# Preparation results of the attention in the attention's own PSUM bank, drained at the head of the next scan part

## The chip, the cores and the metric

The kernel runs on one core of a Trainium2 chip, in one launch. The metric is device time in microseconds (us); the times of a kernel are medians of several runs. A profile is one execution recorded by the hardware profiler. The engines are named as the profile names them: PE (TensorE, matmuls) with PEld (its weight loads), DVE (VectorE), ACT (ScalarE), POOL (GpSimd), and SP, whose queue issues the DMAs.

## What is computed

The input is x, 8 images of 256 channels and 48 x 48 pixels (2304 tokens). Two layers follow one another, each added to its input. Layer 0 is an attention over each token's 16 most similar tokens, layer 1 is two Mamba blocks.

```python
# layer 0: x = x + conv0(gn(x))
feat_pos = tokens @ W.T + bias
feat = feat_pos[:, :, :c]
pos = feat_pos[:, :, c:]
norm = jnp.linalg.norm(pos, axis=-1, keepdims=True)
pos = pos / jnp.maximum(norm, 1e-12)
sim = jnp.einsum('bnc,bmc->bnm', pos, pos)
topksim, topkid = jax.lax.top_k(sim, K)              # K = 16
attn = jax.nn.softmax(topksim, axis=-1)
out = jnp.einsum('bnk,bnkc->bnc', attn, topkfeat)
...
# layer 1: x = x + conv1(gn(x)), for each of DEPTH = 2 blocks
xn = _layernorm(xf, ...)
xi, z = in_proj(xn); xc = silu(conv(xi)); dt, Bm, Cm = x_proj(xc)
dt = jax.nn.softplus(...)
h = h * jnp.exp(dt * A) + dt * B_t * x_t             # over the 2304 tokens
y = jnp.einsum('bds,bs->bd', h, C_t) + xc * Dp
out = (y * silu(z)) @ out_w
```

## The kernel before

**Scan parts.** Layer 1 is the frame of the program. Tokens are cut into 6 chunks of 384, and a chunk of one of the two blocks is a *unit*: 12 units an image. A unit's 512 inner channels with 16 states each are cut into 16 *steps* of 32 channels (128 partitions with four states on each), and a step is scanned in two *parts* of two states. So an image has 384 parts and the program 3072. In each part ACT makes two decays (`decay`, L828, an exponential into one of two pairs of PSUM banks, called `da` in the profile), DVE runs one `tensor_tensor_scan` (L843), and either DVE (L845) or POOL (L871, `pool_part`) multiplies the states with C. POOL makes B times x for each step two steps ahead (L804). `sum_states` (L886, L889) sums the states of four steps over partitions on PE into a tile `y`.

**The order.** The main loop runs over parts m and writes the order out by hand; each engine works through its instructions in that order. A part m holds, in this order: `carry(m - 1)` and `decay(m + 1)`; at an even part POOL's products and `take_up`, at an odd one `carry_pool`; the unit's other pieces that the table `between` gives to this part (`inner`); `run_scan(m)`; the pieces of the table `behind` (`outer`); and last one piece of layer 0, by `ahead.go(m)`. The tables give each piece a part counted from its unit's first, with negative numbers for what comes ahead: input projection (`in_proj`, tile `pe`), the convolution's `tap` and `taps`, `silu_x`, `x_proj`, `softplus` with the step-size matmuls `step_size` (tile `pd`), the copies of z and `silu_z`, the layer norm (`mean`, `variance`, `root`, `root_end`, `spread_root`, `scale`), `gate`, `out_proj` (tile `pw`) and `leave`.

**Layer 0 beside the scan.** `layer0` is a generator; each `yield` ends what it puts into one part. The first image's layer 0 runs alone, before the scan (`alone`). For each of the other seven, `Ahead` runs it while the image before is scanned: it starts 42 parts ahead of that image's first scan (at part 342 of the image still being scanned) and has to be done 384 parts later. It is made of

- the *preparation*: group norm statistics over x (`group_stats`, tiles `pm` and `pv`), then for each chunk two projections `pp` (256 position channels), three feature products `pf`, the squared norms `pn`, and, for the chunk before, the inverse norms spread over all partitions (`spread`, tile `pb`) with which DVE scales `pos` (L298). ACT drains `pp` (L337, and L341 squares), `pf` (L346) and `pn` (L351);
- the *attention*: 18 blocks of 128 tokens by the table `within`, 16 parts apart, starting at a fixed part in 16. The preparation's last `yield` hands over the number of the first part, and `go` waits for the part that fits.

**PSUM.** Of the eight banks four hold decays, three make up the tag `mm`, and one is the tag `po`, in which the attention sums the weighted features of a block (`weigh`, L462). All other matmul results of layer 1 take `mm` (helper `mm`), and so do those of layer 0 (helper `mm0`), which are the preparation's `pm`, `pv`, `pp`, `pf`, `pn`, `pb` and the attention's `psim`, `pt`, `pr`. A matmul that needs a bank of a tag with none free waits until the last reader of the earliest one has gone by.

**When a preparation result is drained.** `step(make, use)` takes a matmul and its drain. It makes the matmul and keeps the drain in `pending`; beside the scan, at most one is kept (`depth` is 1). The next `step`, one part later and again at that part's end, runs the kept drain first and then its own matmul.

Of the kernel before, what the change touches and what calls it, by code (L numbers as in the profile page):

```python
# [8 lines left out]
F32 = mybir.dt.float32  # L9
# [6 lines left out]
P = 128  # L16
# [9 lines left out]
def tile_conv_preact(  # L26
# [19 lines left out]
    B, C, N = x.shape  # L46
# [7 lines left out]
    T = 384  # L54
    NCH = N // T
    TB = T // P
# [125 lines left out]
    def group_stats(st, found, mm0, name):  # L182


        mv = small.tile([P, CB, 2], F32, tag="gn_mv", name=f"mv_{name}")
        for cb in range(CB):
            nc.vector.bn_aggr(mv[:, cb, :], st[:, cb])
        yield
        pm = mm0(CB, f"pm_{name}")
        nc.tensor.matmul(pm, group, mv[:, :, 0], start=True, stop=True)  # L190
        yield
        mean = small.tile([P, CB], F32, tag="gn_mean", name=f"mean_{name}")
        nc.scalar.copy(mean, pm)
        yield
        q = small.tile([P, CB], F32, tag="gn_q", name=f"q_{name}")
        nc.gpsimd.tensor_sub(q, mv[:, :, 0], mean)
        nc.gpsimd.tensor_mul(q, q, q)
        nc.gpsimd.tensor_add(q, q, mv[:, :, 1])
        yield
        yield  # L200
        pv = mm0(CB, f"pv_{name}")
        nc.tensor.matmul(pv, group, q, start=True, stop=True)
        yield
        rstd = small.tile([P, CB], F32, tag="gn_rstd", name=f"rstd_{name}", bufs=4)
        var = small.tile([P, CB], F32, tag="gn_var", name=f"var_{name}")
        nc.scalar.copy(var, pv)
        rsqrt_start(rstd, var, eps5)
        yield
        rsqrt_end(nc.gpsimd, rstd, var, 1e-5, name)
        shift = small.tile([P, CB], F32, tag="gn_shift", name=f"shift_{name}", bufs=4)  # L210
        nc.gpsimd.tensor_mul(shift, mean, rstd)
        nc.gpsimd.tensor_scalar(shift, shift, -1.0, None, ALU.mult)
        found.extend((rstd, shift))
        yield

    def spread(cols, n, psum, name):

        pb = psum(n * P, name)
        for j in range(n):
            nc.tensor.matmul(  # L220
                pb[:, j * P : (j + 1) * P], cols[:, j : j + 1].to_broadcast([P, P]), ident,
                start=True, stop=True,
            )
        return pb
# [2 lines left out]

    def layer0(b, left, pool, ps0, alone):  # L230
        def mm0(w, name):
            return ps0.tile([P, 512], F32, tag="mm", name=name, bufs=5 if alone else 3)[:, :w]

        more = 2 if alone else 1
        depth = 2 if alone else 1
        pending = []

        def step(make, use):

            if len(pending) == depth:  # L240
                leave_psum()
            pending.append((make(), use))

# [5 lines left out]
        st = small.tile([P, CB, NCH, 6], F32, tag="gn_st0", name=f"st0_{b}")  # L249
# [15 lines left out]
            yield  # L265
        found = []
        nxt = load_chunk(pool, x[b], 0, "x", f"xt_{b}_0", 3 * more)
        yield from group_stats(st, found, mm0, f"a{b}")
        rstd, shift = found
        pos = pool.tile([P, CB, N], F32, tag="pos", name=f"pos_{b}", bufs=1)  # L270
        feat = pool.tile([P, NB, C], F32, tag="feat", name=f"feat_{b}", bufs=1)
# [21 lines left out]
        def scale(c):  # L293


            def use(pb):
                cs = slice(c * T, (c + 1) * T)
                nc.vector.tensor_tensor(  # L298
                    pos[:, :, cs], pos[:, :, cs], pb.unsqueeze(1).to_broadcast([P, CB, T]), ALU.mult
                )  # L300

            step(lambda: spread(rn[c], TB, mm0, f"pb_{b}_{c}"), use)

        def chunk(c, xn):
            cs = slice(c * T, (c + 1) * T)

            def project(ob):
                pp = mm0(T, f"pp_{b}_{c}_{ob}")
                for k in range(CB):
                    nc.tensor.matmul(  # L310
                        pp, w0_sb[:, k, C + ob * P : C + (ob + 1) * P], xn[:, k, :],
                        start=(k == 0), stop=(k == CB - 1),
                    )
                return pp

            def features(j):
                pf = mm0(C, f"pf_{b}_{c}_{j}")
                for k in range(CB):
                    nc.tensor.matmul(
                        pf, xn[:, k, j * P : (j + 1) * P], w0_sb[:, k, 0:C],  # L320
                        start=(k == 0), stop=(k == CB - 1),
                    )
                return pf

            def norms():
                pn = mm0(TB, f"pn_{b}_{c}")
                for j in range(TB):
                    for k in range(CB):
                        nc.tensor.matmul(
                            pn[:, j : j + 1], sq[:, k, j * P : (j + 1) * P], ones_col,  # L330
                            start=(k == 0), stop=(k == CB - 1),
                        )
                return pn

            def position(ob):
                def use(pp):
                    nc.scalar.activation(  # L337
                        pos[:, ob, cs], pp, AF.Identity, bias=b_pos[:, ob : ob + 1]
                    )
                    if ob == CB - 1:  # L340
                        nc.scalar.activation(sq, pos[:, :, cs], AF.Square)  # L341

                return use

            def feature(j):
                return lambda pf: nc.scalar.copy(feat[:, c * TB + j, :], pf)  # L346

            def norm(pn):
                n2[c] = small.tile([P, TB], F32, tag="n2", name=f"n2_{b}_{c}")

                nc.scalar.activation(n2[c], pn, AF.Relu, bias=tiny[:, 0:1])  # L351

            for ob in range(CB):
                step(lambda: project(ob), position(ob))
                yield
            if c > 0:
                inverse_norm(c - 1)
            for j in range(TB):
                step(lambda: features(j), feature(j))
                yield  # L360
                if j == 0 and c > 0:
                    inverse_norm_end(c - 1)
            step(norms, norm)
# [3 lines left out]
        for c in range(NCH):  # L367
            yield from chunk(c, xn)
            if c + 1 < NCH:
                xn = normalized(c + 1)  # L370
            yield
            if c > 0:
                scale(c - 1)
                yield
        while pending:
            leave_psum()
# [2 lines left out]
        yield  # L379
        inverse_norm_end(NCH - 1)  # L380
        yield
        yield
        scale(NCH - 1)
        yield
        leave_psum()
        yield
# [131 lines left out]
                f(t, *args)  # L518
            yield
        found = []  # L520
        yield from group_stats(st1, found, mm0, f"b{b}")
        left.update(x1=x1, rstd=found[0], shift=found[1])

    lefts = [{} for _ in range(B)]
    with tc.tile_pool(name="first", bufs=1) as pool0, tc.tile_pool(
        name="first_ps", bufs=1, space=PSUM
    ) as ps0:
        for _ in layer0(0, lefts[0], pool0, ps0, True):
            pass


# [132 lines left out]
    def scale(unit):  # L664
        v = unit["v"]
        nc.vector.tensor_tensor(  # L666
            v, v, unit["lb"].unsqueeze(1).to_broadcast([P, CB, T]), ALU.mult
        )
# [204 lines left out]
    def carry_pool(n):  # L873

        if not 0 <= n < NSTEP:
            return
        unit, i, k = at(n)
        lo = [p for p in range(PARTS) if on_pool(unit, i, p)]
        if lo and unit["c"] + 1 < NCH:
            qs = slice(lo[0] * HQ, (lo[-1] + 1) * HQ)  # L880
            nc.scalar.copy(h_st[:, unit["d"], i, qs], unit["bx"][i][:, qs, T])
# [78 lines left out]
    class Ahead:  # L960
# [3 lines left out]

        def turn(self, image):
            self.image, self.begun, self.started = image + 1, None, False
            self.run = iter(())
            if self.image < B:
                self.run = layer0(self.image, lefts[self.image], keep, ps, False)

        def finish(self, image):
            while self.image <= image:
                for _ in self.run:
                    pass
                self.turn(self.image)

        def go(self, m):
            if self.image == B:
# [9 lines left out]
    ahead = Ahead()  # L988
    first = min(part for part, *_ in between + behind)
    last = max(part for part, *_ in between + behind)  # L990
    for m in range(first, PARTS * NSTEP - HOOKS + last + 1):
        n, p = divmod(m, PARTS)
        carry(m - 1)
        decay(m + 1)
        if p == 0:
            make_bx(n + LEAD)
            pool_part(n - 1)
            take_up(n + 1)
        else:
            carry_pool(n - 1)  # L1000
        for f, unit, args in inner.get(m, ()):
            if f is load_v:
                ahead.finish(unit["b"])
            f(unit, *args)
        run_scan(m)
        for f, unit, args in outer.get(m, ()):
            f(unit, *args)
        ahead.go(m)
# [41 lines left out]
```

## Time and profile before

| | |
|---|---|
| median of 3 runs | 9901.13 us (9897.18 to 9910.42) |
| the profiled execution | 9898.83 us |
| its span | 9897.1 us |
| mean granted PE clock | 0.889 of full speed |
| scan, DVE L843, both forms | 5330.6 us busy, 3072 times |
| decays, ACT L828 | 3591.0 us busy, 6144 times |
| B times x, POOL L804 | 5298.4 us busy, 1536 times |
| products with C, POOL L871 | 3303.6 us busy, 1320 times |
| preparation's drains on ACT, L337, L341, L346, L351 | 160.3 us busy, 336 times |
| preparation's scaling on DVE, L298 | 45.3 us busy, 48 times |

The busy share of an engine is a mean over stages. A row of waits names the instruction that waited, who released it, and the total; a timeline row has the start, the time taken (of the whole run of like instructions, where it says x4), and in brackets how long the engine had been idle before it and for whom. The tail of a name says what is written and read: `pf<-w,xt` is a matmul of weights and tokens into the tile `pf`.

### The profile page before, as it was taken

What the parts mean: (1) busy time and instruction counts of PE and PEld (TensorE: products, weight loads), DVE (VectorE), ACT (ScalarE), POOL (GpSimd) and SP (SyncE); (2) the same over time, 40 slices, a digit from 0 to 9 for tenths busy, and PEclk for the clock granted to TensorE, in tenths of its full rate; (3) what the DMA queues carried; (4) which work ended last, traced back from release to release, by engine and by line L of the source; (5) the groups of instructions that cost most, each with busy time, mean ns of one, the idle gap of its engine ahead of it and who ended that gap; (6) DMA issues with size and microseconds to landing.
All of it is one profiled execution on the core that took longest, in us unless ns stands there. A gap on an engine that the chain in (4) does not pass through costs nothing. (4 is left out here: it accounts for less than half of the span.)

```text
span 9897.1 us, 133780 instructions
## 1 busy us (share of the span) xinstructions
PE 8000.3 (81%) x36736; PEld 4388.5 (44%) x36736; DVE 8956.8 (90%) x7993; ACT 7322.2 (74%) x15966; POOL 8943.3 (90%) x3927
## 2 busy tenths in 40 slices
PE   8878887788878888788877888778887788866665
PEld 6644544444534454445444445344544444522222
DVE  4589998999989999899998999899998999988998
ACT  4477777778777877777877787777787778766766
POOL 0099999999989999899998999999998999999999
PEclk9989998899989998899988999889998899977777
DMA  1144445444444444444454444444445444444544
GB/s 32 37 133 126 134 130 152 124 132 129 136 142 131 129 134 137 140 126 133 130 148 128 130 128 134 144 132 125 135 128 152 121 133 127 138 136 129 145 138 122
DMA packets 1243503, 1271.37 MB, mean 128 GB/s; under 512 B 266592, under 2 KB 1215840, under 8 KB 1242752
## 3 DMA queue, kind: packets, MB, share of 16 engines
q1 hardware_dynamic: 1230496, 1262.45, 44.7%
q8 instruction: 293, 4.80, 0.2%
q14 instruction: 458, 3.75, 0.1%
q10 hardware_dynamic: 12256, 0.36, 0.1%
HBM read 1048.94 MB, written 212.86 MB: 127 GB/s over the span
## 5 line engine op out<-in xcount | busy, mean ns | idle before, releaser
L804 POOL TENSOR_TENSOR bx<-BC,dtxr 128x1536 f32<-128x1536 f32 x1536 | 5298.4, 3453 | 115.6 <-PE y L889 59.8
L828 ACT ACTIVATE da<-dtr,A_sb 128x385 f32<-128x385 f32 x6144 | 3591.0, 585 | 871.6 <-DVE bx L843 558.0
L843 DVE TENSOR_TENSOR_SCAN bx<-da,bx 128x770 f32<-128x770 f32 x2040 | 3521.8, 1746 | 190.5 <-ACT da L828 151.4
L871 POOL TENSOR_TENSOR bx<-bx,BC 128x1536 f32<-128x1536 f32 (+1 forms) x1320 | 3303.6, 2503 | 217.5 <-DVE bx L843 205.4
L843 DVE TENSOR_TENSOR_SCAN da<-da,bx 128x770 f32<-128x770 f32 x1032 | 1808.8, 1753 | 193.4 <-ACT da L828 149.0
L602 PE MATMUL pe<-vn,inw 128*128 128x384 f32 (+1 forms) x3072 | 1258.9, 543 | 394.1 <-DVE xr L924 87.0
L399 PE MATMUL psim<-pos 128*128 128x512 f32 (+1 forms) x2880 | 1370.8, 608 | 183.5 <-ACT sim L408 74.7
L465 PE MATMUL po<-feat,aT 128*128 128x256 f32 x5184 | 1364.0, 412 | 13.8 <-ACT aT L454 7.6
L889 PE MATMUL y<-bx,sel 128*32 128x384 f32 x12288 | 1221.2, 533 | 44.2 <-POOL bx L871 37.9
L465 PEld LDWEIGHTS po<-feat,aT 128*128 128x128 f32 x5184 | 1029.8, 205 | 361.9 <-issue 113.9
L845 DVE TENSOR_TENSOR bx<-da,BC 128x768 f32<-128x768 f32 x1032 | 988.8, 958 | 35.5
L602 PEld LDWEIGHTS pe<-vn,inw 128*128 128x128 f32 x3072 | 590.1, 206 | 902.6 <-issue 191.2
L399 PEld LDWEIGHTS psim<-pos 128*128 128x128 f32 x2880 | 552.8, 206 | 818.8 <-issue 470.8
L889 PEld LDWEIGHTS y<-bx,sel 128*32 128x32 f32 x12288 | 394.1, 118 | 856.6 <-issue 725.0
L702 DVE SCALAR_TENSOR_TENSOR xc<-pe,cw,xc 128x384 f32<-128x384 f32 x1152 | 695.7, 611 | 42.8 <-ACT xc L694 15.7
L732 PE MATMUL pd<-dbl,dtp_sb 16*128 16x384 f32 x768 | 424.3, 668 | 342.0 <-ACT dt L741 209.0
L859 ACT COPY h_st<-da 128x2 f32<-128x2 f32 x832 | 131.7, 158 | 686.4 <-DVE bx L845 680.0
L454 ACT ACTIVATE aT<-pt 128x512 f32<-128x512 f32 (+1 forms) x720 | 388.1, 548 | 245.9 <-PE pt L446 239.8
L445 PE MATMUL pt<-ident,sim 128*128 128x128 f32 x2592 | 539.6, 291 | 33.7 <-DVE v L666 17.6
L907 PE MATMUL pw<-z,ow 128*128 128x384 f32 x1536 | 531.5, 499 | 15.0 <-DVE v L666 7.0
L437 ACT ACTIVATE rest<-left,three 128x512 bf16<-128x512 f32 (+1 forms) x720 | 467.0, 670 | 59.7 <-DVE left L422 59.7
L446 PE MATMUL pt<-minus,rest 128*128 128x128 bf16 x2592 | 491.6, 225 | 3.2 <-ACT rest L437 3.2
(146 smaller groups left out, 9766.8 us busy)
## 6 DMA issues: line engine op xcount, KB each, us to landing
dtxr<-dtx_d SPq DMA_DIRECT2D x6144, 48.0 KB, 1.8
dtr<-dt_d SPq DMA_DIRECT2D x6144, 48.0 KB, 1.8
BC<-bc_d SPq DMA_DIRECT2D x768, 192.0 KB, 3.7
inw<-in_in_wT_dram SPq DMA_DIRECT2D x768, 128.0 KB, 2.2
dtx_d<-dtx SPq DMA_DIRECT2D x384, 192.0 KB, 2.0
dt_d<-dt SPq DMA_DIRECT2D x384, 192.0 KB, 2.2
ow<-in_out_wT_dram SPq DMA_DIRECT2D x96, 512.0 KB, 4.0
dmat<-diag SPq DMA_DIRECT2D x384, 64.0 KB, 2.3
```

Of the source, the lines that this page charges most:

```text
L399: nc.tensor.matmul(pm, pos[:, k, t * P : (t + 1) * P], pos[:, k, c0 : c0 + w], start=(k == 0), stop=(k == CB - 1),)
L445: nc.tensor.transpose(pt[:, q], row["sim"][:, r], ident)
L465: nc.tensor.matmul(row["po"], aT[:, m % PT, :], feat[:, m, :], start=(m == 0), stop=(m == NB - 1))
L602: nc.tensor.matmul(pe, w[:, k], unit["vn"][:, k, lo:], start=(k == 0), stop=(k == CB - 1))
L702: nc.vector.scalar_tensor_tensor(unit["xc"][e], unit["pe"][e][:, k : k + T], cw[:, unit["d"], e, k : k + 1], unit["xc"][e], ALU.mult, ALU.add,
L804: nc.gpsimd.tensor_tensor(bx[:, :, 1:], unit["BC"][0], unit["dtxr"][i].unsqueeze(1).to_broadcast([P, Q, T]), ALU.mult,)
L828: nc.scalar.activation(da[:, s * (1 + T) : (s + 1) * (1 + T)], unit["dtr"][i], AF.Exp, scale=A_sb[:, unit["d"], i, p * HQ + s : p * HQ + s ...
L843: nc.vector.tensor_tensor_scan(h, da, g, 0.0, ALU.mult, ALU.add)
L845: nc.vector.tensor_tensor(bx[:, :, 0:T], da.rearrange("p (q t) -> p q t", q=HQ)[:, :, 1:], unit["BC"][1][:, qs], ALU.mult,)
L871: nc.gpsimd.tensor_tensor(g[:, :, 0:T], g[:, :, 1:], unit["BC"][1][:, qs], ALU.mult)
L889: nc.tensor.matmul(y[j * G : (j + 1) * G, :], sel, unit["bx"][k * J + j][:, q, 0:T], start=False, stop=True, skip_group_check=True,)
L907: nc.tensor.matmul(pw, unit["ow"][:, k, cb * P : (cb + 1) * P], unit["z"][k], start=(k == 0), stop=(k == DB - 1),)
```

## The change

The preparation's helper becomes `front`: alone it is `mm0` as before, beside the scan it takes a tile of the tag `po`, which has one bank. `group_stats`, both before and after the attention, uses it too. The list `pending` is handed in by `Ahead`, whose new method `use` runs one kept drain; the main loop calls it in each part after `carry`, `decay`, POOL's products and `take_up` or `carry_pool`, and ahead of the `inner` pieces. `step` therefore finds nothing to drain when it is called beside the scan. The scaling by `pb` doesn't go through `pending` there: its matmul is made in one part, and DVE's multiplication follows at the end of the next, after which one further part passes before the next chunk's projection. An empty `yield` ahead of the last scaling goes.

```diff
-    def layer0(b, left, pool, ps0, alone):
+    def layer0(b, left, pool, ps0, alone, pending):
         def mm0(w, name):
             return ps0.tile([P, 512], F32, tag="mm", name=name, bufs=5 if alone else 3)[:, :w]
 
+        def front(w, name):
+            if alone:
+                return mm0(w, name)
+            return ps0.tile([P, 512], F32, tag="po", name=name, bufs=1)[:, :w]
+
         more = 2 if alone else 1
-        depth = 2 if alone else 1
-        pending = []
 
         def step(make, use):
 
-            if len(pending) == depth:
+            if len(pending) == 2:
                 leave_psum()
             pending.append((make(), use))
...
-            step(lambda: spread(rn[c], TB, mm0, f"pb_{b}_{c}"), use)
+            if alone:
+                step(lambda: spread(rn[c], TB, front, f"pb_{b}_{c}"), use)
+                return
+            made = spread(rn[c], TB, front, f"pb_{b}_{c}")
+            yield
+            use(made)
...
-                pp = mm0(T, f"pp_{b}_{c}_{ob}")
+                pp = front(T, f"pp_{b}_{c}_{ob}")
...
             if c > 0:
-                scale(c - 1)
+                yield from scale(c - 1)
                 yield
...
         inverse_norm_end(NCH - 1)
         yield
-        yield
-        scale(NCH - 1)
+        yield from scale(NCH - 1)
         yield
         leave_psum()
...
         def turn(self, image):
             self.image, self.begun, self.started = image + 1, None, False
-            self.run = iter(())
+            self.run, self.pending = iter(()), []
             if self.image < B:
-                self.run = layer0(self.image, lefts[self.image], keep, ps, False)
+                self.run = layer0(self.image, lefts[self.image], keep, ps, False, self.pending)
...
+        def use(self):
+            if self.pending:
+                made, use = self.pending.pop(0)
+                use(made)
...
             carry_pool(n - 1)
+        ahead.use()
         for f, unit, args in inner.get(m, ()):
```

`pf`, `pn`, `pm` and `pv` change from `mm0` to `front` in the same way as `pp`.

More of the change, by code (lines that the diff above doesn't have):

```diff
@@ L267, in layer0 @@
         nxt = load_chunk(pool, x[b], 0, "x", f"xt_{b}_0", 3 * more)
-        yield from group_stats(st, found, mm0, f"a{b}")
+        yield from group_stats(st, found, front, f"a{b}")
         rstd, shift = found
@@ L316, in features @@
             def features(j):
-                pf = mm0(C, f"pf_{b}_{c}_{j}")
+                pf = front(C, f"pf_{b}_{c}_{j}")
                 for k in range(CB):
@@ L325, in norms @@
             def norms():
-                pn = mm0(TB, f"pn_{b}_{c}")
+                pn = front(TB, f"pn_{b}_{c}")
                 for j in range(TB):
@@ L520, in layer0 @@
         found = []
-        yield from group_stats(st1, found, mm0, f"b{b}")
+        yield from group_stats(st1, found, front, f"b{b}")
         left.update(x1=x1, rstd=found[0], shift=found[1])
@@ L527, in tile_conv_preact @@
     ) as ps0:
-        for _ in layer0(0, lefts[0], pool0, ps0, True):
+        for _ in layer0(0, lefts[0], pool0, ps0, True, []):
             pass
```

## The prediction

> **What bounds the kernel now.** I read the page first (busy shares).
>
> ```profile
> span 9897.1 us, 133780 instructions
> PE 8000.3 (81%) x36736; PEld 4388.5 (44%) x36736; DVE 8956.8 (90%) x7993; ACT 7322.2 (74%) x15966; POOL 8943.3 (90%) x3927
> ```
>
> DVE and POOL carry the kernel, both at 90%. The change touches the preparation alone, so I next took busy times by stretch: one image's preparation (from part 342 of an image to part 21 of the next; parts are counted from an image's first scan) and the attention that follows such a stretch (parts 29 to 334).
>
> ```profile
> 5127.90:5339.10 211.20, 156.29 (x678) 84.39 (x677) 174.06 (x164) 149.35 (x319) 180.25 (x130) 0.83 0.50 145
> 5361.60:6298.10 936.50, 810.12 (x3820) 451.88 (x3820) 896.81 (x793) 730.05 (x1604) 914.99 (x342) 0.93 0.46 131
> ```
>
> Columns: stretch and length, then PE, PEld, DVE, ACT and POOL busy, clock, DMA share, GB/s. In the attention POOL is busy 98% and DVE 96%; in the preparation 85% and 82%. The most that could come from there is 211.2 - 180.3 (POOL's work) = 31 us an image. There are seven such stretches, the first partly ahead of the scans: I count 6.5, so 200 us at the very most. The table of waits for that stretch names what the idle time waits for (total us, times, longest):
>
> ```profile
> DVE da L843 <- ACT da L828: 12.3, 5, 5.7
> ...
> ACT pos L337 <- PE pp L310: 9.2, 4, 3.5
> ...
> ACT n L351 <- PE pn L329: 6.2, 4, 2.6
> ...
> DVE pos L298 <- PE pb L220: 5.8, 2, 4.0
> ...
> PE pf L319 <- ACT feat L346: 4.2, 2, 2.9
> ...
> PE pp L310 <- ACT z L761: 2.6, 1, 2.6
> ```
>
> The scans wait for their decays (L828), which ACT makes in program order; ACT in turn stands at drains (`pos`, `n`) whose matmuls are late, and PE is late at the last two lines because it waits for a drain that frees a bank. Last, the timeline around parts 1 to 4, where the sum will be decided (start, length, engine, line):
>
> ```profile
> 5265.81 1.68 POOL L871 TENSOR_TENSOR bx<-bx,BC 128x768 f32<-128x768 f32 x1
> ...
> 5267.67 1.49 PE L886 MATMUL y<-xc,dmat 128*128 128x384 f32 x2
> ...
> 5268.87 1.75 DVE L843 TENSOR_TENSOR_SCAN bx<-da,bx 128x770 f32<-128x770 f32 x1
> 5269.09 2.99 PE L889 MATMUL y<-bx,sel 128*32 128x384 f32 x32
> 5269.28 0.24 ACT L162 ACTIVATE rs<-lv,eps 128x3 f32<-128x3 f32 x1
> ...
> 5270.54 0.15 DVE L178 SCALAR_TENSOR_TENSOR lv<-lv,nt_rs 128x3 f32<-128x3 f32 x1
> ...
> 5271.01 1.76 DVE L843 TENSOR_TENSOR_SCAN da<-da,bx 128x770 f32<-128x770 f32 x1
> ...
> 5272.00 2.85 PE L310 MATMUL pp<-xt,w 128*128 128x384 f32 x8
> ...
> 5273.60 0.58 ACT L337 ACTIVATE pos<-pp,b_pos 128x384 f32<-128x384 f32 x1 [3.54 <-PE pp L310]
> ...
> 5275.37 1.76 DVE L843 TENSOR_TENSOR_SCAN bx<-da,bx 128x770 f32<-128x770 f32 x1 [1.15 <-ACT da L828]
> ```
>
> POOL finishes the last state product at 5267.5, PE sums states (`y`) until 5272.1, and only then makes `pp`, for which ACT waits 3.5 us. The layer norm's root (L162) stands ahead of that drain on ACT, so DVE goes on with its Newton step (L178) and the scan at 5271.0.
>
> **What the Trainium skill says.** PSUM — Partial Sum Buffer, "Engine vs sequencer instructions": the ScalarE, VectorE and GpSimdE queues are strict FIFO, and matmuls start and complete in program order. The trace agrees: the decay behind the 3.54 us wait moved with it. The same page, "PSUM bank collisions raise a hardware error", has PSUM guarded by semaphore per bank: with one bank a matmul can't start before the drain of the result before. The trace shows that as `pf` waiting 2.9 us for `feat`. Perfetto Trace Analysis, "Optimization Strategy": the same gap repeating on an engine that should be saturated can mean too little PSUM for the next tile. Here the gaps repeat in every preparation (5.7 us before the scan of part 376 in each of six images).
>
> **The change part by part.** No instruction is added or removed; the matmuls and drains have the durations of their rows.
> 1. *Removed*: preparation results no longer take one of the three `mm` banks. The build's order shows fewer waits on PE: in the stretch walked below, of the four step-size matmuls `pd` only the last waits for ACT, where before each did, and the `y` of part 362 loses its wait for ACT.
> 2. *Moved*: a drain goes from the end of the next part to its head. ACT stands there after the decays of the next part, ahead of that part's own work (copies, root, silu, softplus) and of the decays after that. PE gets no slack part any more.
> 3. *Added*: one part more for each of five `pb` results. 64 parts become 69; in the kernel before, attention began at part 29 after seven empty parts, so it begins at 29 again with two left. The attention stays as it is, at no cost. From chunk 1 on, each step meets other scan work than before, by one part more after each `pb`. The xt loads move with it; SP's queue can then stand behind a later `pf`, some 2 us by the place of `pf22`, covered by the replicated loads' lead of about five parts.
>
> I walked the queues by hand through the stretch at 5128 to 5340, with these rows' durations, and compare when the same scan starts (minus is earlier).
> - *Parts 358 to 370.* `pp` needn't wait 2.6 us for the copy of z; ACT reaches the silu 1.6 us sooner. But silu with its two table loads (4.4 us), then normal and norm are ACT's own work: 1.3 is left at part 364, 0.4 at 368. At 370 `pn1` now stands at the head, behind `y` (3.6 us) and its own 1.5, ahead of the silu, which starts as before. Sum -0.1.
> - *Parts 371 to 380.* Softplus ran from 5234.2 to 5241.0 with waits of 1.26 and 0.70 for `pd`; with free banks only about 0.4 remains. A 1.42 us drain moves ahead of it, and rn (0.5) takes the place of feat (0.37): -1.0. Then `pf22` comes out behind `y` and its head waits 2.1 us, which costs 1.3. Sum +0.3.
> - *Parts 0 to 5.* Now `n3` is the drain at the head of part 2, and its matmul `pn3` stands behind `y`. POOL's 5267.5 bounds `y`, so it ends near 5271.3 in any case, `pn3` (1.5) at 5272.8. The root (0.7) is behind that head, then DVE's Newton step (0.47): the scan of 5271.0 starts at about 5274.0. DVE, in order, has nothing else. The old gaps of 0.55, 1.15 and 0.51 go, so of 3.0 there remain +2.4.
> - *Parts 6 to 12.* The 4.0 us that DVE waited for `pb3` go. In return `pf40` stands behind `pw` (5.3 us) and a `pe` (1.5) and its head waits 2.6; decays of parts 9, 10 and 11 come late by 1.4, 0.9 and 5.6, where the old gaps were 0.8, 4.0, 1.4 and 2.9. Sum -0.4.
> - *Parts 13 to 20.* The 1.2 us (DVE at `pb`) goes. `pn5` stands behind `y`, which took 5.5 us at the low clock here; the head before the silu waits for it: the silu would start 1.9 later. Sum +1.5.
>
> Sum per image: -0.1 + 0.3 + 2.4 - 0.4 + 1.5 = +3.7, by 6.5 gives +24, I take 25. On the profiled execution's 9898.8 us (its span is 9897.1) that is 9924; the median of the three runs, 9901.1, lies 2.3 higher: 9926.
>
> Bounds: a head drain costs nothing if PE leads by its whole queue, and up to the 4.2 us found at part 2 if it is behind a `y`; the freed banks are worth between nothing and the gaps that carry them, 13 us an image. That is 22 less 9: DVE's gaps in the timeline, as means of six images, are 6.6 us at parts 360 to 363, 0.7 at 371, 1.6 at 375 (5.7 less the 4.1 that softplus shows at part 23, where nothing is prepared), 7.8 at 381 to 8 and 5.5 at 10 to 15; the last image, which prepares nothing, still shows about 4.6 a unit at the silu and the gate, for two units 9. For the likeliest case I let each place err by about 1.5 us: +-3.5 an image, +-23 us.
>
> **The rivals.**
> - *The banks win.* PE runs ahead, so that heads find their results; about 9 of the 13 us are kept: -9 x 6.5 = -59, 9842. For it: five bank waits vanish from PE's order. Against it: `y` is bound by POOL, not by banks.
> - *They cancel.* The two errors meet: 9901, no difference. About what a measurement can tell from none is 0.2%, 20 us.
> - *Head drains pile up.* As forecast, but the late decays also delay h_st copies and POOL's products, which keep 85% busy here with 31 us of room, and the seam at parts 22 to 26, which had no preparation, gets `pb5` ahead of softplus' gap of 4.1: +8 an image, +52, 9953. It decides once more than three heads per image wait over 2 us.
> - *The change doesn't do what it says*, and the attention begins 16 parts later because 69 parts don't fit: excluded by the count, two parts are left.
>
> **How the numbers follow.** Chances: forecast 0.50, banks win 0.28, cancel 0.12, pile up 0.10. The forecast's own range is 9903 to 9949; the bound of 9921 cuts it so that 0.31 of its 0.50 is slower and 0.19 the same. Slower: 0.31 + 0.10 = 0.41. Same: 0.19 + 0.09 of the cancelling = 0.28. Faster: 0.28 + 0.03, the cancelling's early tail = 0.31. The range 9838 to 9958 takes in the faster case's centre and the pile-up's; some 0.12 lies below it and 0.05 above.
>
> **What would show it.** Right: with the same instruction counts, ACT `n` L351's wait for PE `pn` grows at parts 2 and 18, and DVE gets a new wait of 3 to 4 us at L178 on ACT; DVE's wait for `pb` and `pd`'s for `dt` shrink; parts 29 to 334 take 936 us as before. Wrong: the preparation takes less than 209 us, or the attention's length changes.

## The result, and the profile after

The changed kernel takes 9944.51 us (median of 4 runs, 9938.08 to 9949.55) against 9901.99 us before: ratio 1.0042, 95% interval 1.0024 to 1.0059. It is slower by about 42 us. The profiled execution took 9938.08 us, 39.2 us more than that of before. The first two lines of its page (busy us, share of the span, instructions) show little:

```profile
span 9936.3 us, 133724 instructions
...
PE 8045.1 (81%) x36736; PEld 4400.7 (44%) x36736; DVE 8958.2 (90%) x7993; ACT 7325.8 (74%) x15966; POOL 8944.2 (90%) x3927
```

Each engine has the instructions it had. DVE, ACT and POOL have the busy time they had to within 4 us; PE, at 81%, is busy 45 us more. On the engines that carry the kernel the 39 us are waits. Busy times by stretch, for the same image as before the change (the preparation, then the attention):

```profile
5167.40:5380.00 212.60, 159.23 (x673) 83.03 (x671) 173.23 (x163) 150.01 (x319) 178.22 (x124) 0.81 0.51 143
5403.30:6337.60 934.30, 808.82 (x3820) 450.82 (x3820) 896.70 (x793) 729.94 (x1604) 915.16 (x342) 0.93 0.48 131
```

The attention is untouched: the mean of seven images is 935.2 us, 934.9 before. What this image shows of the preparation, +1.4 us, is less than the mean; the starts of the scans give the whole account. The first scan starts at 537.4 us, where it was 517.7: **+19.7 us before any scan has run**. From the first to the last scan it is 9384.6 us against 9364.6: **+20.0 us**, in the preparations.

What DVE waited for over the whole run (us in total, times, longest):

```profile
DVE bx L850 <- ACT da L835: 192.6, 208, 6.4
...
DVE pos L301 <- PE pb L220: 52.8, 8, 25.8
...
DVE lv L178 <- ACT nt_rs L177: 35.4, 22, 4.8
```

The same rows of the kernel before:

```profile
DVE bx L843 <- ACT da L828: 151.4, 186, 3.1
...
DVE pos L298 <- PE pb L220: 73.7, 19, 15.7
```

The wait for `pb` fell by 21 us; that of the scans into `bx` for their decays rose by 41, and L178, the Newton step of the layer norm's root, waits 35.4 us where it waited 4.6. What the feature products `pf` and their copies waited for shows why. First the kernel before, then the changed one (idle time of PE until it could make `pf`, then who waited for it; us, times):

```profile
  ACT feat L346: 27.4, 14
...
  ACT feat L346: 7.3, 14
```

```profile
  ACT feat L354: 56.6, 55
...
  ACT feat L354: 84.7, 49
```

PE waits for the copy of the product before it twice as long as it did, and ACT waits for the product, now at the head of its part, almost twelve times as long. The stretch that the prediction showed, parts 1 to 4, in the timeline of the changed kernel:

```profile
5310.30 1.68 POOL L878 TENSOR_TENSOR bx<-bx,BC 128x768 f32<-128x768 f32 x1
...
5311.96 2.80 PE L896 MATMUL y<-bx,sel 128*32 128x384 f32 x32
...
5314.69 1.50 PE L337 MATMUL pn<-ones_col,w 128*128 128x1 f32 x12
...
5316.28 0.26 ACT L359 ACTIVATE n<-pn,tiny 128x3 f32<-128x3 f32 x1 [2.60 <-PE pn L337]
...
5316.44 0.26 ACT L162 ACTIVATE rs<-lv,eps 128x3 f32<-128x3 f32 x1
...
5317.27 0.17 DVE L178 SCALAR_TENSOR_TENSOR lv<-lv,nt_rs 128x3 f32<-128x3 f32 x1 [3.45 <-ACT nt_rs L177]
```

`pn3` stands behind `y`, its drain on ACT waits 2.6 us for it, the root (L162) stands behind that drain, and DVE is idle for 3.45 us. The mean gap of six images is 4.0 us.

### The profile page after: what moved, and what is told of

Read it like the earlier page. It is cut to its first block, busy times and chain, and to the rows that moved or that the text cites. A ratio compares the mean times of both kernels' runs of the same rounds, so it can differ in the third digit from the quotient of the medians.

```text
span 9936.3 us, 133724 instructions
## 1 busy us (share of the span) xinstructions
PE 8045.1 (81%) x36736; PEld 4400.7 (44%) x36736; DVE 8958.2 (90%) x7993; ACT 7325.8 (74%) x15966; POOL 8944.2 (90%) x3927
## 5 line engine op out<-in xcount | busy, mean ns | idle before, releaser
L739 PE MATMUL pd<-dbl,dtp_sb 16*128 16x384 f32 x768 | 437.3, 690 | 316.2 <-ACT dt L748 175.7
```

## The experiments

All edits are against the changed kernel unless said otherwise. In the tables "first scan" and "scans" (first to last) are of each kernel's profiled execution, ratios are against the kernel before, measured beside it.

**The halves apart.** The change does three things: another bank, another place for the drains, five more parts. `bank_only` is the kernel before with `front` alone:

```diff
+        def front(w, name):
+            if alone:
+                return mm0(w, name)
+            return ps0.tile([P, 512], F32, tag="po", name=name, bufs=1)[:, :w]
...
-                pp = mm0(T, f"pp_{b}_{c}_{ob}")
+                pp = front(T, f"pp_{b}_{c}_{ob}")
```

> The kernel before, with the preparation's results in the po bank but each drained where it was, at the end of the next part just ahead of the next matmul, and no added parts. Theory (the drain's place at the head costs, the freed mm banks help): faster than before by about 0.2 to 0.4%, 9860 to 9885 us, the scan of part 376 waits about 1 us less, no new wait at the root's Newton step at part 2; the first scan starts near 518 us if the head drains made it late. Rival (one bank alone costs, as each matmul must wait for the drain just ahead of it): slower by 0.1 to 0.4%, with the first scan near 537 us.

`head_only` is the changed kernel with the banks of before:

```diff
-            return ps0.tile([P, 512], F32, tag="po", name=name, bufs=1)[:, :w]
+            return mm0(w, name)
```

> The changed kernel with the preparation's results back in the three mm banks; drains at the head and the added parts stay. Theory: the head drains cost as in the changed kernel, and without free banks PE leads less, so slower than before by 0.4 to 0.7%, 9940 to 9975 us, with DVE's wait of 3 to 4 us at part 2. Rival (the one bank is what costs): near the time before, 9890 to 9915 us.

`shift_only` is the kernel before with the five parts alone:

```diff
                 scale(c - 1)
                 yield
+                leave_psum()
+                yield
```

> The kernel before, with only the five added parts: after each of the five pb results DVE's scaling comes in the next part and one part more passes; mm banks and drains at the end of the next part stay. Theory: the shift only moves which scan work a step meets; within 0.2% of before, 9885 to 9920 us, first scan within 3 us of 517.7. Rival (the shift sets the loss): slower by 0.3 to 0.5%, 9930 to 9950 us, and no wait over 2 us at part 2 without the head drain.

| kernel | time us | ratio (95%) | first scan | scans |
|---|---|---|---|---|
| before | 9900.13 | | 517.7 | 9364.6 |
| `bank_only` | 9980.66 | 1.0080 (1.0068 to 1.0093) | 543.7 | 9419.9 |
| `head_only` | 9995.08 | 1.0095 (1.0079 to 1.0110) | 524.4 | 9460.0 |
| `shift_only` | 9890.79 | 0.9990 (0.9982 to 0.9998) | 520.9 | 9353.8 |

Each half costs more alone than the whole change. For the bank the theory fell: it was to be the gain, and it costs 80 us. The early drains cost 95 us, above the forecast of 40 to 75, and 104 against `shift_only`, which has the same added parts. The timeline of `bank_only` at parts 361 to 363 shows what the bank costs:

```profile
5252.56 1.28 ACT L771 ACT_TABLE_LOAD   x1
...
5255.59 1.28 ACT L775 ACT_TABLE_LOAD   x1
5256.89 0.37 ACT L351 COPY feat<-pf 128x256 f32<-128x256 f32 x1
...
5257.31 2.08 PE L324 MATMUL pf<-w,xt 128*128 128x256 f32 x4 [5.61 <-ACT feat L351]
...
5260.60 2.91 PE L894 MATMUL y<-bx,sel 128*32 128x384 f32 x32
...
5263.74 0.56 DVE L900 TENSOR_TENSOR z<-y,z 128x384 f32<-128x384 f32 x1 [8.74 <-PE y L894]
```

With one bank, `pf` must wait for the copy of the `pf` before it. That copy stands at the end of ACT's part, behind the silu and its two table loads, so PE stands 5.6 us at `pf`. The `y` behind it in program order is late, and DVE's gate, which needs that `y`, waits 8.7 us. The timeline of `head_only` at parts 360 and 361 shows the other half:

```profile
5245.33 0.54 DVE L931 TENSOR_TENSOR xr<-xr,pw 128x384 f32<-128x384 f32 x1
...
5245.98 2.90 PE L318 MATMUL pp<-xt,w 128*128 128x384 f32 x4 [5.91 <-issue]
...
5248.91 0.58 ACT L345 ACTIVATE pos<-pp,b_pos 128x384 f32<-128x384 f32 x1 [6.73 <-PE pp L318]
...
5251.00 1.77 DVE L850 TENSOR_TENSOR_SCAN da<-da,bx 128x770 f32<-128x770 f32 x1 [5.12 <-ACT da L835]
```

PE starts `pp` 0.11 us after DVE has read `pw` (L931), which I read as `pp` waiting for that bank; the profile names no releaser, so this is not shown. ACT stands at the head drain of this `pp` for 6.7 us, and the next decay and scan behind it. In the changed kernel the same `pp` has its own bank and its drain waits 0.78 us. So the two halves need each other: the early drain keeps the single bank from stopping PE for long, and the own bank keeps the early drain from waiting, on that reading, for the scan's banks. The added parts gain 9 us on their own.

**The preparation ahead of the first scan.** `lead_old` prepares the second image, and no other, in the old way:

```diff
+        old = alone or b == 1
+        if old:
+            pending = []
+
         def front(w, name):
-            if alone:
+            if old:
                 return mm0(w, name)
...
```

> The changed kernel, but the second image's preparation, the one that runs while the first scans are still being prepared, works as before (mm banks, drains at the end of the next part, no added parts). Theory: of the 39 us by which the profiled execution grew, the 19.7 us ahead of the first scan go, and the 3.7 us that this image gained at its parts 0 to 22 are lost; 9925 to 9932 us, first scan near 518 us. Rival (the late start is only moved on, since the scans then wait for what the preparation still owes): first scan near 518 us but the total within 5 us of the changed kernel's 9944.

It took 9935.10 us, ratio 1.0032 (1.0020 to 1.0045), with the first scan at 522.1 us, 15.3 us earlier than after the change; 4.6 us of it were given back in the first image's parts 0 to 22. Some 10 us of the loss are ahead of the first scan. There the first unit goes through its layer norm, projection and convolution step by step, with no scan running, and the preparation's matmuls and drains stand between those steps. The timeline of the changed kernel:

```profile
469.61 2.93 PE L318 MATMUL pp<-xt,w 128*128 128x384 f32 x4 [0.82 <-ACT xt L283]
...
473.21 2.93 PE L318 MATMUL pp<-xt,w 128*128 128x384 f32 x4 [0.67 <-ACT pos L345]
...
476.18 0.58 ACT L345 ACTIVATE pos<-pp,b_pos 128x384 f32<-128x384 f32 x1 [3.02 <-PE pp L318]
...
478.93 0.37 ACT L354 COPY feat<-pf 128x256 f32<-128x256 f32 x1 [1.29 <-PE pf L327]
...
481.46 0.37 ACT L354 COPY feat<-pf 128x256 f32<-128x256 f32 x1 [2.16 <-PE pf L327]
481.73 1.30 ACT L686 ACTIVATE vn<-v,nbias,nw 128x384 f32<-128x384 f32 x2
```

And that of `lead_old`, where the matmuls come in one run each and ACT reaches the unit's own work (`vn`) 6.0 us after the first `pp` and not 12.1:

```profile
471.68 4.38 PE L322 MATMUL pp<-xt,w 128*128 128x384 f32 x8 [0.76 <-ACT xt L287]
...
475.90 2.75 PE L331 MATMUL pf<-w,xt 128*128 128x256 f32 x12
...
477.71 1.30 ACT L692 ACTIVATE vn<-v,nbias,nw 128x384 f32<-128x384 f32 x2
```

`lead_old` takes away the bank, the early drains and the added parts together; the first two experiments tell them apart. `head_only` has the early drains and the added parts, and at this place it looks like `lead_old`: the matmuls run together, `vn` comes 6.4 us after the first `pp`, and the first scan starts at 524.4 us.

```profile
470.32 4.40 PE L318 MATMUL pp<-xt,w 128*128 128x384 f32 x8 [0.76 <-ACT xt L283]
...
476.76 1.31 ACT L686 ACTIVATE vn<-v,nbias,nw 128x384 f32<-128x384 f32 x2
```

`bank_only` has the single bank with late drains. There the matmuls stand apart as in the changed kernel, `vn` comes 9.6 us after the first `pp`, and the first scan starts at 543.7 us. So it is the single bank that makes the start late, and not the place of the drains.

**The root at part 2.** `root_first` puts the head drain behind the inner pieces in the parts that hold the root:

```diff
-        ahead.use()
+        late = any(f is root for f, *_ in inner.get(m, ()))
+        if not late:
+            ahead.use()
         for f, unit, args in inner.get(m, ()):
...
             f(unit, *args)
+        if late:
+            ahead.use()
```

> The changed kernel, with the head drain put behind the inner pieces in those parts whose inner pieces hold the layer norm's root. Theory (the head drain of n3 at part 2 stands ahead of the root and costs DVE's Newton step L178 about 3 to 4 us in each image): that gap goes, the stretch of parts 1 to 5 falls from 16.2 us to about 12 to 13, and the time by 2.5 to 3 us x 6 to 7 images = 15 to 20 us, to about 9925 to 9930. Rival (the loss at parts 1 to 5 is only taken over from a later place, DVE being ahead of ACT there): parts 1 to 5 gain 3 us and parts 5 to 12 give it back; within 5 us of 9944.

It took 9943.60 us, ratio 1.0047 (1.0035 to 1.0060): nothing gained, and not by the rival's way either, since the gap was still there. Its timeline:

```profile
5311.91 0.24 ACT L162 ACTIVATE rs<-lv,eps 128x3 f32<-128x3 f32 x1
...
5315.25 0.26 ACT L359 ACTIVATE n<-pn,tiny 128x3 f32<-128x3 f32 x1 [2.86 <-PE pn L337]
5315.41 0.20 ACT L177 ACTIVATE nt_rs<-rs 128x3 f32<-128x3 f32 x1
...
5315.64 0.17 DVE L178 SCALAR_TENSOR_TENSOR lv<-lv,nt_rs 128x3 f32<-128x3 f32 x1 [4.44 <-ACT nt_rs L177]
```

My edit had moved only half: the first step of the root (L162) now ran 3.3 us before the drain, but its last step on ACT (L177) belongs to `root_end`, a piece of the table `behind`, and still stood behind the drain. `root_end_first` moves the drain behind both, to the end of the part:

```diff
             f(unit, *args)
+        if late:
+            ahead.use()
         ahead.go(m)
```

> The changed kernel, with the head drain moved to the end of the part, behind both halves of the layer norm's root, in those parts that hold the root (one part in 32; of the preparation that is part 2 with n3, and part 354). Moving it behind the first half alone left DVE's gap before L178 at 3.9 us, since ACT's last step of the root (L177) stands in the second half, behind the drain still. Theory: now L177 no longer waits for pn3; the gap of 4.0 us before L178 falls below 1 us, parts 1 to 5 from 16.2 us to about 13, the time by 3 us x 6.5 = 20 us, to about 9924. Rival (the delay is only handed on: pb3 and with it DVE's scaling and the next pp come later): the gap goes and parts 5 to 12 grow by as much; within 6 us of 9944.

It took 9912.14 us, ratio 1.0012 (1.0006 to 1.0019), 32 us less than the changed kernel. The timeline at the same place:

```profile
5297.65 0.20 ACT L177 ACTIVATE nt_rs<-rs 128x3 f32<-128x3 f32 x1
5297.89 0.17 DVE L178 SCALAR_TENSOR_TENSOR lv<-lv,nt_rs 128x3 f32<-128x3 f32 x1 [0.56 <-ACT nt_rs L177]
...
5298.18 1.50 PE L337 MATMUL pn<-ones_col,w 128*128 128x1 f32 x12
...
5299.72 0.26 ACT L359 ACTIVATE n<-pn,tiny 128x3 f32<-128x3 f32 x1 [1.86 <-PE pn L337]
```

The drain still waits 1.86 us for `pn3`, but DVE has its root by then. The wait at L178 is 0.6 to 2.1 us in the six images. Parts 1 to 5 fall from 16.15 to 13.68 us, parts 5 to 12 from 26.37 to 26.19: nothing is handed on. The scans take 9364.8 us, as before the change.

**Both places.** `root_lead_old` is `root_first` and `lead_old` together, `root_end_lead` is `root_end_first` and `lead_old` together.

> The two separate costs taken away together: the preparation of the second image, ahead of the first scan, as in the kernel before, and the head drain behind the root. If the two are independent places, their gains add: 10 us (measured alone) and 15 to 20 us (expected of the root), so 9944 - 27 = about 9917, first scan at 522 us. If the root's gain is only moved to a later place, 9930 to 9937.

> As root_end_first, and the second image's preparation, ahead of the first scan, as in the kernel before. Theory: the two are separate and add: first scan at about 522 us, 9944 - 20 - 10 = about 9914, which leaves some 15 us against the kernel before for the late heads at parts 367, 378, 1, 8 and 19. Rival: 9930 to 9937, if the root's delay is only handed on.

| kernel | time us | ratio (95%) | first scan | scans |
|---|---|---|---|---|
| after | 9944.51 | 1.0042 (1.0024 to 1.0059) | 537.4 | 9384.6 |
| `root_lead_old` | 9927.62 | 1.0030 (1.0018 to 1.0041) | 520.8 | 9392.2 |
| `root_end_first` | 9912.14 | 1.0012 (1.0006 to 1.0019) | 537.9 | 9364.8 |
| `root_end_lead` | 9901.06 | 1.0001 (0.9993 to 1.0009) | 521.2 | 9365.2 |

With both places mended the change costs nothing against the kernel before, which is more than I expected (9914). The two add up: the old preparation ahead of the first scan gives 11.1 us here and gave 9.4 alone; beside `root_first` it gave 16.0.

**Two more.** `piece_first` puts the preparation's matmul at the head of the part too, right behind the drain:

```diff
         ahead.use()
+        early = ahead.begun is None and ahead.image < B
+        if early:
+            ahead.go(m)
...
-        ahead.go(m)
+        if not early:
+            ahead.go(m)
```

> The changed kernel, with the preparation's matmul put at the head of the part too, right behind the drain of the one before, so that it has a whole part until the next head. Theory (what the single bank costs is that a matmul comes out at a part's end behind y, pe or pw, so that the next head drain waits for it on ACT): ACT's waits for pp, pf and pn fall, the loss against the kernel before goes, 9870 to 9905. Rival (PE, in order, then stands at the bank until ACT's head drain has gone by, and the matmuls of the scans behind it start late): DVE waits move to y and pd, 9940 or more.

It took 10104.53 us, ratio 1.0211 (1.0197 to 1.0225). The rival was right, and larger than it said. Its waits in the same image's preparation:

```profile
POOL bx L811 <- PE y L896: 34.7, 4, 14.2
...
DVE pos L301 <- PE pb L220: 16.7, 4, 6.8
PE pf L327 <- ACT feat L354: 15.4, 7, 5.5
PE pp L318 <- ACT pos L345: 15.3, 5, 4.4
DVE z L902 <- PE y L896: 13.7, 2, 10.3
```

PE now stands at the single bank for 31 us in this stretch, with the scan's `y` behind it, and POOL (34.7 us) and DVE (13.7) wait for `y`.

`shift_late` is `shift_only` with the added parts from the third image on (`if b > 1`). `two_turns` adds the attention's bank to it, by turns with the three, drains at the end:

```diff
+        turns = [0]
+
+        def front(w, name):
+            turns[0] += 1
+            if alone or turns[0] % 2:
+                return mm0(w, name)
+            return ps0.tile([P, 512], F32, tag="po", name=name, bufs=1)[:, :w]
```

> The kernel before, with only the five parts added, and these only from the third image on: what runs ahead of the first scan is left as it was. Theory (the shift of the chunks against the scan's pieces is worth about 12 us in the scans and costs 3.6 us ahead of the first scan): first scan at 517.7 us as before, time 9886 to 9890. Rival (the gain of the shift was of the second image's own place or chance): 9895 to 9902.

> The kernel before with the added parts (from the third image on) and its drains at the end of the next part, but with the preparation's results by turns in a bank of the three and in the attention's bank, so that no result waits for the drain of the one just before it. Theory (it is the single bank's strict turn, matmul after drain, that costs 80 us when the drains stand at the end; the bank itself, as a fourth, is worth a little): 9875 to 9890, the waits of pf for feat and of pp for z go. Rival (a bank that is waited for at all, or its order, costs): above 9900. If free banks are worth nothing in this order: 9888 to 9893, as the added parts alone.

`shift_late` took 9890.60 us, 0.9993 (0.9985 to 1.0001); its first scan started at 522.8 us, though nothing ahead of it differs from the kernel before, so that start varies by about 5 us between executions. `two_turns` took 9902.51 us, 1.0001 (0.9993 to 1.0009), as its rival had it (above 9900): 12 us more than `shift_late`. What its `pf` waited for, and who waited for it, over the whole run:

```profile
  ACT feat L354: 0.8, 2
...
  ACT feat L354: 58.8, 37
```

PE's wait for the copy before it is gone (38.7 us in `shift_late`), and it bought nothing: ACT waits for `pf` 58.8 us, 44.5 in `shift_late`. A fourth bank by turns is not what this kernel lacks. The two kernels with the added parts alone are the fastest here, by 9 us or 0.1%; only `shift_only` has its whole interval below 1. `root_end_lead` (9901.06) has the added parts too, so by the medians its bank and drains still cost what the parts gain; the intervals overlap.

## Why the prediction was right, and where it was not

The forecast was 9926 us, slower by 25; it is slower by 42. The direction holds, and so does the mechanism that I named as deciding. The loss is made of two terms: the later preparations, whose sum I had nearly right, and the one ahead of the first scan, which I had hardly seen.

| us an image, mean of six | forecast | after less before | `shift_late` less before |
|---|---|---|---|
| parts 358 to 370 | -0.1 | -0.04 | +0.27 |
| 370 to 380 | +0.3 | +3.33 | +2.70 |
| 380 to 5 | +2.4 | +3.50 | -0.20 |
| 5 to 12 | -0.4 | -2.10 | -2.62 |
| 12 to 20 | +1.5 | -0.75 | -1.60 |
| sum | +3.7 | +3.95 | -1.44 |

That +3.7 came so near to +3.95 is luck: three of the five terms are off by 1.7 to 3.0 us and cancel. The last column has the added parts without the bank and the early drains. Against it these two cost 5.4 us an image, of which 3.7 lie at parts 380 to 5.

- **Parts 0 to 5: right.** The head drain of `n3` behind `y`, ahead of the root: +2.4 forecast and a new wait of 3 to 4 us at L178; the wait is 4.0 us. `root_end_first` shows that this place is the cause, by taking it away. In its profile it is worth 2.5 us an image at parts 1 to 5 and 19.8 us in the scans, by the medians 32 us in all. Most of the difference lies in the executions that were profiled: that of the changed kernel was its fastest, 6.4 us below its median, and that of `root_end_first` was 6.4 us above its own.
- **The first preparation: the term that failed.** I counted 6.5 images, the one ahead of the first scan as half a stretch of the same price, so some +2 us. In profiles with three banks and late drains there the first scan starts at 517.7 to 522.8 us, in those with the changed preparation (after, `root_first`, `root_end_first`) at 533.2 to 537.9: 15 us, of which 9 to 16 stay in the time. The single bank makes them, as `bank_only` (543.7) and `head_only` (524.4) show: matmul and drain take turns, the first unit's steps stand behind them, and no scan runs that could hide it. Without this term the forecast of 25 stands against some 26 to 33.
- **Parts 371 to 380 and 5 to 20: the sum was near, its terms were not.** Of the late heads that I priced, `pf40` behind `pw` waits 2.65 us (forecast 2.6), `pf22` behind `y` 4.35 (2.1), and `pn5` ahead of the silu only 0.49 (1.9; in three of the seven images it is 1.81). But the last column shows that the five added parts alone, with old banks and old drains, give most of what happened here: +2.7 at 370 to 380, where DVE's gap ahead of part 376's scan grows to 6.9 us, and -4.2 at 5 to 20, where its waits at `pb` (4.0 and 1.2 us) go. I had counted those waits as freed, and for the parts added only that the attention stays as it is; that is true, but where the chunks come to lie had a price of its own.
- **The freed banks.** I bounded them between nothing and a gain of 13 us an image. The own bank costs without the early drains (80 us), and a bank more by turns gains nothing. The bound should have reached below nothing. The trace agrees with what the Trainium skill says (PSUM — Partial Sum Buffer, "Engine vs sequencer instructions": strict order on ACT and DVE, program order of matmuls): in `bank_only` PE stood 5.61 us at `pf`, and the `y` behind it kept the gate waiting for 8.74 us, though that `y` did not need the bank.
- **The rivals.** "The banks win" is refuted by `bank_only` and `two_turns`. "Head drains pile up" is what happens without the own bank (`head_only`, drains waiting 6.7 us, seven to nine of them over 2 us an image). In the changed kernel exactly three heads wait over 2 us in each of the six images, and it was to decide from more than three. By its number alone, 9953, it lies nearer to the result than the forecast does. "They cancel" came out for the scans once the root was freed.
- **The signs.** As forecast, DVE's waits for `pb` (73.7 to 52.8 us over the run) and those of `pd` for `dt` (209.0 to 175.7) shrank, the attention kept its length, and `n` waits 2.2 to 3.0 us in part 2. Not as forecast: the other late `n`, at part 17 or 18, waits only 0.5 to 1.8 us, less than it did at part 14 before (2.2 to 2.6), so that ACT's wait for `pn` fell from 43.9 to 33.9 us over the run.

Not tried: the own bank and the early drains without the added parts; two banks for the attention's tag, which would leave `mm` two.

## What to carry to other kernels

A drain moved to the head of an engine's part delays all that the engine does after it, so look for the one short chain that another engine waits for (here a layer norm's root, in two pieces) and keep the drain behind the whole of it: moving half the chain gained nothing. Here one bank for a series of results was bearable only where the drain came early, and an early drain only where its matmul had a bank of its own; neither half could be judged alone. Price a change of this kind where nothing runs beside it, too: ahead of the main loop the single bank cost more than the whole change did in any stretch of the loop. And take out the side effects by themselves: the added parts, which I had counted as free, were worth 9 us.

## What the runs showed of the hardware

In the series matmul, drain, matmul ahead of the first scan the matmuls themselves took twice as long: four `pp` 2.93 us and four `pf` 2.07 us, against 1.45 to 1.56 and 1.02 to 1.13 us some 15 us later. The granted clock in and after that stretch (start and length, busy times in the order used above, clock) was 0.55 and 0.87:

```profile
440.00:480.00 40.00, 17.51 (x44) 10.73 (x45) 12.60 (x36) 8.03 (x20) 4.27 (x21) 0.55 0.44 141
480.00:500.00 20.00, 17.83 (x68) 11.89 (x66) 6.78 (x12) 10.79 (x24) 1.01 (x5) 0.87 0.17 47
```

The series did not bring the clock down: from 460 to 470 us it was 0.50 in the kernel before, too. It kept it from rising. From 465 to 485 us the clock was 0.50 in the changed kernel and in `bank_only`, and 0.75 to 0.79 in the kernel before, `lead_old` and `head_only`, where the same matmuls run together; of the eight `pp` shown for `lead_old` (4.38 us) the first four took 2.93 us and the others only 1.45.

The Trainium skill (TensorE: Matmul & The Clock Gate, "Part 1: The HAM clock gate") has PE at half its clock until it has been busy for about 3.4 us on end. These numbers fit roughly: from the first `pp` on the clock came back after some 3 us in `lead_old` and some 6 us in the kernel before. There is one point to add: the idle times between were only 0.46 to 0.67 us, each for a drain, and they were enough to keep the clock low over five matmul groups of 2 to 3 us each. Once it was high, the same did no harm: from 490 to 500 us in the changed kernel it was 1.00, with two idle times of 0.46 us. So ahead of the first scan a bank's turn cost not only the wait but the speed of the matmuls around it.
